# Four graph layers on one core: the diagonal of 15 row tiles multiplied by itself, and three or four column tiles whole there in place of six

## The chip, the core and the metric

The kernel runs on one core of a Trainium2 chip. The metric is the device time of one execution in microseconds (us). Three runs of the kernel before took 1402.44, 1414.2 and 1417.59 us; the median is 1414.2 us. A further execution was recorded by the hardware profiler, and every duration below comes from that one.

## What is computed

There are 2708 nodes with 512 features each, and one 2708 x 2708 matrix `adj` (float32, 45848 entries that are not zero, the whole diagonal among them, and denser towards low row and column numbers). Four layers follow one another; each begins with `h = relu(layernorm(x))` and ends with `x = x + layer(h)`:

```python
# layer 0: rows of adj plus a normalised mask, times h
head = (adj > 0) / sqrt(count of adj > 0 in the row)
inc  = adj + head;  out = (inc @ h) / inc.sum(-1)
# layer 1: attention with scores masked by (1 - max(adj, I)) * 1e16: in effect one node is picked per row
# layer 2: two graph convolutions and a projection
h = relu(adj @ (x @ W1) + b1);  h = relu(adj @ (h @ W3) + b3);  out = tanh(h @ Wf + bf)
# layer 3: mean over the nonzero pattern
A = (adj != 0);  out = (A @ (x @ W + b)) / A.sum(0)
```

So `adj`, or its pattern, is multiplied four times with a 2708 x 512 matrix.

## The kernel before

The nodes are cut into 22 row tiles of 128 (the last, number 21, has 20 rows). For a row tile m the product with `adj` has two parts. The first DENSE = 6 column tiles are taken **whole**: blocks of 128 x 128 are loaded from the transposed matrix and multiplied with the first six tiles of the right-hand side. Of the other columns only those that have an entry in any of the 128 rows are taken. They stand in a **list** for each row tile, cut in chunks of 128 (the table `CHUNKS`, 130 chunks in all): for each chunk GpSimd issues one indirect DMA that gathers the 128 entries of the matrix (`ac`, L576) and, in each later stage, one that gathers the 128 rows of the right-hand side (`gg`, L953; 256 KB each). Row tile 0 takes all columns whole. A list that doesn't fit sets a flag (`bad`, L406), and then a slow general path (from L1364) runs in addition.

The stages, in order, each a loop over row tiles:

- **Stage 0** (about 0 to 515 us): layer 0 and the lists. `row_norm` (L519) and `row_sum` (L537) read a slab of `adj` on ScalarE (ACT) three times: signs, their count, and a copy in place that sums the row. `count` (L265) adds up, on TensorE (PE), for three row tiles at once which columns are occupied; `rank_blocks` (L316) scans that on VectorE (DVE), the ranks are stored to HBM and loaded back spread over 128 partitions (`load_ranks`, L354), and `search` (L369) finds the listed columns. `attended` (L549) does the work of layer 1 on the slab. `incidence` (L627) builds `adj + head` from the blocks `at` and from the list; then PE multiplies (L791, float32), and `after` (L728) projects (`yacc`, L158).
- **Stage 1a** (about 515 to 650 us): `first_product` (L1066) for all 22 tiles, each with three products in float32r of four matmuls each (`project3`, L905), and row tile 0 of the first convolution.
- **Stage 1b** (about 650 to 950 us): the loop `for m in order_m` (L1096): `aggregate` (L957) and `aggregated` (L1024) for the other tiles, then one `project3` (L918).
- **Stage 2** (about 950 to 1310 us): the loop `for m in order_2` (L1285): the second convolution, again `aggregated`, then `project3` with Wf, tanh, the residual, a layernorm, and `project3` with W for layer 3; the result `go` is stored to `hid` (L1317) and without the first six tiles to `hidr` (L1320). Row tiles 1 to 5 come last.
- **Stage 3** (about 1310 to 1492 us): layer 3. Row tiles 0 to 3 take all columns whole (`full_steps`, L1252), the others six whole tiles (`whole_h`, L1200) and the list (`listed_products`, L1213; gathers from `hidr`). Each right-hand tile is split in two float32r halves, so each whole tile or chunk is two matmuls (L1193).

In stages 1b and 2 a whole tile is split in three float32r parts (`a_hi`, `a_lo`, `a_s`, L989 to L991) and costs three matmuls (L1002); a chunk of the list is one float32 matmul (L1005, two records in the profile). After the last one the two banks are added and the bias follows (`sum_banks` L879 and L880, then L1030), and `relu_parts` (L889) transposes the sum `u` on PE (L893).

What sets the order: each engine works through its own fixed list of instructions, written out by a scheduler ahead of time, and waits on semaphores. SyncE (SP) issues nearly all plain DMAs in one such list. Buffers come from pools: eight `gg` buffers for gathered rows, three `raw` for loaded blocks, two `u` (which in stage 2 hold the sum `u` and the tensor `z` in turn), two each of `agg`, `aggs`, `v_hi`, `v_lo`, `v_s`, and one each of `main` and `mixed`.

Of the kernel before, what the change touches and what calls it, by code (L numbers as in the profile page):

```python
# [9 lines left out]
FP = mybir.dt.float32  # L10
# [27 lines left out]
LEAD = 3  # L38
CHUNKS = (0, 10, 9, 8, 7, 7, 7, 7, 6, 6, 6, 6, 6, 6, 6, 5, 6, 5, 5, 5, 5, 2)


@with_exitstack
def kernel(
# [46 lines left out]
    def dense_of(m):  # L90

        return 0 if m == NT - 1 else DENSE

# [14 lines left out]
    hid = dram.tile([N + 1, D], FP, name="hid")  # L108
    hidr = dram.tile([N + 1 - DENSE * P, D], FP, name="hidr")
    y = dram.tile([N, D], FP, name="y")  # L110
# [15 lines left out]
    NGROUP = (NT + GROUP - 1) // GROUP  # L126
    BEHIND = DENSE * P
    WIDE, LOW = (N - BEHIND) // 4, BEHIND // 2
    assert WIDE * 4 == N - BEHIND and WIDE < BLK and LOW * 2 == BEHIND
    cnt_b = dram.tile([NGROUP + 1, P, WIDE], BF, name="cnt_b")  # L130
# [13 lines left out]

    rdeg = const.tile([P, NT], FP, name="rdeg")
    ones_b = const.tile([P, 1], BF, name="ones_b")
    nc.gpsimd.memset(ones_b, 1.0)
# [24 lines left out]

    def norm(pool, xt, n, dst, func=AF.Identity):

        stats = pool.tile([P, nc.vector.BN_STATS_DIM], FP, name="stats")
        nc.vector.bn_stats(stats[:n], xt[:n])
        mv = pool.tile([P, nc.vector.BN_AGGR_DIM], FP, name="mv")
        nc.vector.bn_aggr(mv[:n], stats[:n])
        rstd = pool.tile([P, 1], FP, name="rstd")
        nc.scalar.activation(rstd[:n], mv[:n, 1:2], AF.Sqrt, bias=eps[:n])  # L180
        nc.vector.reciprocal(rstd[:n], rstd[:n])
        shift = pool.tile([P, 1], FP, name="shift")
        nc.vector.tensor_scalar(
            shift[:n], mv[:n, 0:1], rstd[:n], -1.0, op0=ALU.mult, op1=ALU.mult
        )
        nc.scalar.activation(dst[:n], xt[:n], func, scale=rstd[:n], bias=shift[:n])
# [39 lines left out]
    with tc.tile_pool(name="l0_slab", bufs=2) as slabs, tc.tile_pool(  # L226
# [10 lines left out]
        for gd in (h0d, g1d, g2d, hid):  # L237
            nc.gpsimd.dma_start(out=gd[N:], in_=zero)
        nc.gpsimd.dma_start(out=hidr[N - DENSE * P :], in_=zero)

# [11 lines left out]
        for d in range(QUAD, P, QUAD):  # L252
            nc.vector.tensor_add(ahead_of[:, d:], ahead_of[:, d:], ident[:, : P - d])

        place_i = hp.tile([P, NCH], I32, name="place_i")
# [9 lines left out]
        def count(masks):  # L265

            ms = list(masks)
            r, g = len(ms), NGROUP if ms[0] == 0 else ms[0] // GROUP
            for num, w, first, dst in ((2, LOW, 0, cnt_l), (4, WIDE, BEHIND, cnt_b)):
                bank = ps_list.tile([P, BLK], FP, name="list")  # L270
                for b in range(num):
                    c0 = first + b * w
                    for i, m in enumerate(ms):
                        n = rows(m)
                        nc.tensor.matmul(
                            bank[b * QUAD : (b + 1) * QUAD, :w],
                            counts[:n, m % GROUP, :],
                            masks[m][:n, c0 : c0 + w],
                            start=(i == 0),
                            stop=(i == r - 1),  # L280
                        )
                k = num * QUAD
                t = hp.tile([P, w], BF, name=f"counts{num}")
                nc.scalar.copy(t[:k], bank[:k, :w])
                pending_c.append(
                    lambda t=t, k=k, dst=dst: nc.sync.dma_start(out=dst[g, :k], in_=t[:k])
                )
            return t

        def degrees():  # L290
# [4 lines left out]
            for t in range(NT):  # L295
# [7 lines left out]
                )  # L303
            nc.vector.reciprocal(rdeg[:, :NFULL], deg[:, :NFULL])
            if TAIL:
                nc.vector.reciprocal(rdeg[:TAIL, NFULL:], deg[:TAIL, NFULL:])

        def load_counts(g, r, dst):

            for num, w, first, src in ((2, LOW, 0, cnt_l), (4, WIDE, BEHIND, cnt_b)):  # L310
                nc.sync.dma_start(
                    out=dst[:, first : first + num * w].rearrange("i (b w) -> i b w", b=num),
                    in_=src[g, : num * QUAD].rearrange("(b i) w -> i b w", b=num)[:r],
                )

        def rank_blocks(ms, last_block):  # L316

            rk = hp.tile([P, WIDE], HF, name="rk")  # L320
            sums, offs = (wp.tile([P, 1], FP, name=name) for name in ("sums", "offs"))
# [6 lines left out]
            nc.vector.tensor_tensor_scan(rk, rk, rk, offs[:, 0:1], ALU.add, ALU.max)  # L328
            nc.sync.dma_start(out=rank_b[ms[0] // GROUP], in_=rk)

        def rank_rows(ms):
# [12 lines left out]
            if first:  # L344
                nc.sync.dma_start(
                    out=rank_b[m // GROUP].rearrange("(b i) w -> i b w", b=4)[:r],
                    in_=rank[:, first:].rearrange("i (b w) -> i b w", b=4),
                )
            else:
                nc.sync.dma_start(out=rank_l, in_=rank)  # L350
# [3 lines left out]
        def load_ranks(m):  # L354
            first = dense_of(m) * P
            num = N - first
            if first:
                ranks = slabs.tile([P, N + 1 - BEHIND], HF, name="ranks", bufs=2)
                q = m % GROUP

                row = rank_b[m // GROUP].rearrange("(b i) w -> i b w", b=4)[q : q + 1]
                nc.sync.dma_start(
                    out=ranks[:, :num].rearrange("p (b w) -> p b w", b=4),
                    in_=row.to_broadcast([P, 4, WIDE]),
                )
            else:
                ranks = in_slab()[:, : N + 1]
                nc.sync.dma_start(out=ranks[:, :N], in_=rank_l.to_broadcast([P, N]))
# [54 lines left out]
        def norm_h0(ts):  # L423
            for t in ts:
                n = rows(t)
                norm(wp, h0[t], n, h0[t], AF.Relu)
                nc.gpsimd.dma_start(out=h0d[span(t)], in_=h0[t][:n])
# [87 lines left out]
        def row_norm(m):  # L515
# [17 lines left out]
            if m not in LATE:  # L533
                flag_negative(m, sum_sgn, cnt)
            masks[m], row[m] = sgn, (rn, deg, cnt)

# [65 lines left out]

        PIECE0 = 6
        tiles_d = list(range(DENSE))
# [21 lines left out]
        def incidence(m):  # L626
# [20 lines left out]
            if m >= LEAD:  # L647
                pieces = [tiles_d] if dense_of(m) else []
            else:
                pieces = in_order if m + 1 < LEAD else dense_last  # L650
            for ts in pieces:
# [3 lines left out]
                add_head(inc[d], at[d], k, len(ts))  # L655
                pairs += [(inc[:k, i, :n], h0[t][:k]) for i, t in enumerate(ts)]
            if m >= LEAD:
                ac, gs = gathers.pop(m)
# [120 lines left out]
        for m in range(NT):  # L779
# [3 lines left out]
            if m + 2 < NT and m + 2 >= LEAD and dense_of(m + 2):  # L783
                blocks[m + 2] = load_block(m + 2, tiles_d)
            flush()
# [78 lines left out]

    order_2 = order_m[:1] + order_m[DENSE:] + order_m[1:DENSE]
    x3_last = dram.tile([P, D], FP, name="x3_last")
# [94 lines left out]
    def aggregate(m, parts, shifted, gd, marked):  # L961
# [13 lines left out]
        if num:  # L975
            ac = load_listed(m)
            chunks = [(ac[:, c, :], g) for c, g in enumerate(gather(m, gd))]
            if marked:
                mark(whole, ac)
        for ts in dense if dense_of(m) else []:  # L980
            gs = [parts(t) for t in ts]
# [12 lines left out]
            for i, t in enumerate(ts):  # L994
                ghi, glo, gs_ = gs[i]
                first, last = t == 0, t == DENSE - 1
                for acc, a, b, st, sp in (
# [26 lines left out]
    def aggregated(m, parts, shifted, gd, bias, marked=False):  # L1024
        n = rows(m)
        u = wp.tile([P, D], FP, name="u")
        main, mixed = aggregate(m, parts, shifted, gd, marked)
        if dense_of(m):
            sum_banks(u, main, mixed, n)
            nc.vector.tensor_add(u[:n], u[:n], bias[:n])  # L1030
        else:
# [167 lines left out]

    def whole_h(m, t0=0, t1=DENSE):  # L1200

        n = rows(m)
        t1 = min(t1, dense_of(m))
        for ts in (range(t, min(t + PIECE, t1)) for t in range(t0, t1, PIECE)):
            mask = ap.tile([P, PIECE, P], FR, name="a_hi" if t1 - t0 > 1 else "a_s")
            nc.vector.tensor_copy(
# [6 lines left out]
    def listed_products(m):  # L1213
# [4 lines left out]
        for c, g in enumerate(listed_h.pop(m)):  # L1218
            high = part_room()
            if m == order_3[0]:  # L1220

                behind(high[:1, :1], halves[DENSE - 2][0][:1, :1].bitcast(FP))
            for half in split_h(high, g, P):
# [59 lines left out]
    order_3.insert(NT // 2, NFULL)  # L1283
    FIRST = 2
    for m in order_2:  # L1285
        n = rows(m)
# [3 lines left out]
        if dense_of(m) and m not in FULL:  # L1290
            nc.vector.tensor_scalar_add(
                idx_h[:, m, : CHUNKS[m]], idx_g[:, m, : CHUNKS[m]], float(-DENSE * P)
            )
# [23 lines left out]
        nc.sync.dma_start(out=hid[span(m)], in_=go[:n])  # L1317
        if m >= DENSE:
            r0 = (m - DENSE) * P
            nc.sync.dma_start(out=hidr[r0 : r0 + n], in_=go[:n])  # L1320
        elif m == order_2[-1]:
# [3 lines left out]
            nc.vector.tensor_tensor(lo, go, hi.bitcast(FP), ALU.subtract)  # L1325
            halves[m] = hi, lo


# [3 lines left out]
    for k in order_3[:AHEAD]:  # L1332
        if k not in marks:
            gather_h(k)
        whole_h(k, 0, DENSE - 1)
    for i, m in enumerate(order_3):
        listed_products(m)
        if i < AHEAD:
            whole_h(m, DENSE - 1)
        finish_h(m)  # L1340
# [449 lines left out]
```

## Time and profile before

| what | value |
|---|---|
| median of three runs | 1414.2 us (1402.44 to 1417.59) |
| profiled execution | span 1491.9 us from first to last instruction; the page gives no other time for it |
| busy: PE, DVE, ACT, POOL (GpSimd) | 1301.6, 948.3, 689.1, 662.4 us |
| mean granted TensorE clock | 0.944 |
| DMA | 349.04 MB, 234 GB/s over the span |
| matmuls of whole tiles L1002 | 756 records (3 x 252) |
| matmuls of lists L1005 | 520 records (260 matmuls) |
| stage 0 matmuls L791, whole and listed | 348 and 222 records (174 and 111 matmuls) |

The profiled execution is 77.7 us (5.5%) longer than the median. Times are microseconds from the start of the span. A row of the timeline gives start, duration, engine, source line, operation, result<-operands and the number of instructions merged. A matmul's duration runs from its start to its modelled end, and the next one starts before that end; so the distance between two starts, not the duration, is what a matmul costs PE while it is never without work. In a table by stretches each engine has its busy time and, in brackets, its instructions, followed by granted clock, DMA share and GB/s.

### The profile page before, as it was taken

What the parts mean: (1) busy time and instruction counts of PE and PEld (TensorE: products, weight loads), DVE (VectorE), ACT (ScalarE), POOL (GpSimd) and SP (SyncE); (2) the same over time, 40 slices, a digit from 0 to 9 for tenths busy, and PEclk for the clock granted to TensorE, in tenths of its full rate; (3) what the DMA queues carried; (4) which work ended last, traced back from release to release, by engine and by line L of the source; (5) the groups of instructions that cost most, each with busy time, mean ns of one, the idle gap of its engine ahead of it and who ended that gap; (6) DMA issues with size and microseconds to landing.
All of it is one profiled execution on the core that took longest, in us unless ns stands there. A gap on an engine that the chain in (4) does not pass through costs nothing.

```text
span 1491.9 us, 15610 instructions
## 1 busy us (share of the span) xinstructions
PE 1301.6 (87%) x4478; PEld 774.6 (52%) x4478; DVE 948.3 (64%) x1944; ACT 689.1 (46%) x1051; POOL 662.4 (44%) x673
## 2 busy tenths in 40 slices
PE   4868777598898838988999999899999999879997
PEld 2323333243343326755665666466577666556766
DVE  4657777688899668743443445456566655558676
ACT  5856464353444446532323334245445544445453
POOL 1254454666585432044444443233433444535662
PEclk9988988899999869999999999899999999979999
DMA  9986787879798387466777777755565565748885
GB/s 341 349 272 223 243 289 256 295 233 332 226 328 317 107 288 261 157 198 218 244 235 215 239 236 235 262 167 170 161 196 164 180 210 185 226 134 280 271 248 165
DMA packets 196872, 349.04 MB, mean 234 GB/s; under 512 B 22198, under 2 KB 109840, under 8 KB 193045
## 3 DMA queue, kind: packets, MB, share of 16 engines
q1 hardware_dynamic: 149177, 200.80, 40.4%
q0 software_dynamic: 46032, 145.05, 31.2%
q10 hardware_dynamic: 1568, 2.10, 0.4%
q8 instruction: 37, 0.61, 0.2%
q14 instruction: 58, 0.48, 0.1%
HBM read 284.58 MB, written 63.29 MB: 233 GB/s over the span
## 4 chain that ended last, share of the span: by engine, by line
PE 68%; DMA 9%; DVE 7%; issue 7%; ACT 3%; another core or an unknown queue 2%; POOL 2%; SPq 1%; ACTq 0%; DVEq 0%; POOLq 0%
PE aggs L1005 14%; PE main L918 10%; PE acc L791 9%; PE agg L1002 7%; PE mixed L918 5%; PE aggs L1002 4%; PE yacc L158 3%; PE aggs L1193 3%; PE agg L1193 3%; PE pt L893 3%; PE aggs L1017 1%; PE pt L1193 1%; DMA lst<-ac 1%; PE agg L918 1%
## 5 line engine op out<-in xcount | busy, mean ns | idle before, releaser
L1005 PE MATMUL aggs<-gg,ac 128*128 128x512 f32 (+1 forms) x520 | 232.2, 594 | 3.6 <-DMA gg<-g1d,idx_g 3.6
L953 POOL DMA_INDIRECT gg<-g2d,idx_g x130 | 130.9, 1007 | 224.9 <-PE aggs L1005 175.7
L953 POOL DMA_INDIRECT gg<-g1d,idx_g x130 | 133.8, 1029 | 180.4 <-PE aggs L1005 109.3
L576 POOL DMA_INDIRECT ac<-in_adj_t_dram,idx_a x130 | 134.9, 1037 | 132.2 <-DMA lst<-ac 63.1
L791 PE MATMUL acc<-h,inc 128*128 128x512 f32 (+1 forms) x348 | 164.6, 615 | 18.1 <-DVE inc L644 10.3
L1005 PEld LDWEIGHTS aggs<-gg,ac 128*128 128x128 f32 (+1 forms) x520 | 97.6, 189 | 110.0 <-issue 102.2
L594 POOL DMA_INDIRECT h<-h0d,idx_g x111 | 115.3, 1038 | 51.7 <-issue 26.7
L158 PE MATMUL yacc<-wvo,hT 128*128 128x512 f32 (+1 forms) x176 | 92.8, 675 | 46.6 <-ACT hT L193 25.4
L1002 PE MATMUL agg<-ghi,a_hi 128*128 128x512 f32 x252 | 114.9, 456 | 8.6 <-ACT ghi L197 4.4
L989 ACT ACTIVATE a_hi<-raw 128x384 fp32r<-128x384 f32 x84 | 43.6, 520 | 160.5 <-issue 96.0
L791 PEld LDWEIGHTS acc<-h,inc 128*128 128x128 f32 (+1 forms) x348 | 64.9, 195 | 94.8 <-issue 78.8
L791 PE MATMUL acc<-h,incl 128*128 128x512 f32 (+1 forms) x222 | 103.5, 614 | 0.0
L1002 PE MATMUL agg<-glo,a_lo 128*128 128x512 f32 x252 | 101.8, 404 | 0.0
L1002 PE MATMUL aggs<-gs,a_s 128*128 128x512 f32 x252 | 100.2, 401 | 1.0 <-DVE gs L204 1.0
L990 DVE TENSOR_TENSOR a_lo<-raw,a_hi 128x384 fp32r<-128x384 f32 x84 | 47.4, 564 | 76.5 <-ACT a_hi L989 39.8
L899 DVE SCALAR_TENSOR_TENSOR v_lo<-pt,v_hi 128x512 fp32r<-128x512 f32 (+1 forms) x88 | 56.8, 664 | 48.9 <-issue 25.3
L158 PEld LDWEIGHTS yacc<-wvo,hT 128*128 128x128 f32 (+1 forms) x176 | 35.8, 213 | 97.6 <-issue 67.1
L953 POOL DMA_INDIRECT gg<-hidr,idx_h x62 | 63.0, 1016 | 49.8 <-PE aggs L1193 17.2
L880 DVE SCALAR_TENSOR_TENSOR u<-aggs,u 128x512 f32<-128x512 f32 x42 | 28.9, 687 | 77.3 <-PE aggs L1005 64.7
L898 ACT ACTIVATE v_hi<-pt 128x512 fp32r<-128x512 f32 (+1 forms) x88 | 49.1, 579 | 53.7 <-PE pt L893 38.5
L791 PEld LDWEIGHTS acc<-h,incl 128*128 128x128 f32 (+1 forms) x222 | 42.8, 196 | 52.3 <-issue 51.0
L556 DVE MAX8 top<-ar 128x8 f32<-128x2708 f32 (+1 forms) x22 | 65.4, 2972 | 0.1
(321 smaller groups left out, 2829.0 us busy)
## 6 DMA issues: line engine op xcount, KB each, us to landing
ar<-in_adj_dram SPq DMA_DIRECT2D x27, 1354.0 KB
raw<-in_adj_t_dram SPq DMA_DIRECT2D x122, 192.0 KB
slot<-x SPq DMA_DIRECT2D x41, 256.0 KB
at<-in_adj_t_dram SPq DMA_DIRECT2D x27, 384.0 KB
ranks<-rank_b SPq DMA_DIRECT2D x20, 485.0 KB
ac<-lst SPq DMA_DIRECT2D x16, 384.0 KB
h<-in_x_dram SPq DMA_DIRECT2D x21, 256.0 KB
h0d<-h POOLq DMA_DIRECT2D x21, 256.0 KB
```

Source lines behind the costliest of these rows:

```text
L158: nc.tensor.matmul(acc[:n], hT[:, c, :n], w[:, c, :], start=(c == 0), stop=(c == NCD - 1))
L556: nc.vector.max(top[:n], ar[:n])
L576: nc.gpsimd.indirect_dma_start(out=ac[:, c, :n], out_offset=None, in_=adj_units, in_offset=bass.IndirectOffsetOnAxis(ap=idx_a[:, m, c0 + c ...
L594: nc.gpsimd.indirect_dma_start(out=g, out_offset=None, in_=h0d[:, :], in_offset=bass.IndirectOffsetOnAxis(ap=idx_g[:, m, c : c + 1], axis=0),)
L791: nc.tensor.matmul(acc[:n], a, g, start=(i == 0), stop=(i == len(pairs) - 1))
L898: nc.scalar.activation(hi[d], pt[d], AF.Relu, scale=UP)
L899: nc.vector.scalar_tensor_tensor(lo[d], pt[d], 0.0, hi[d].bitcast(FP), op0=ALU.max, op1=ALU.subtract)
L918: nc.tensor.matmul(acc[:n], a[:, c, :n], b[:, c, :], start=first and c == 0, stop=last and c == NCD - 1,)
L953: nc.gpsimd.indirect_dma_start(out=gs[c], out_offset=None, in_=gd[:, :], in_offset=bass.IndirectOffsetOnAxis(ap=index[:, m, c : c + 1], ax ...
L1002: nc.tensor.matmul(acc[:n], a[:k, i, :n], b[:k], start=st, stop=sp)
L1005: nc.tensor.matmul(mixed[:n], a, g, start=(c == 0 and not dense_of(m)), stop=(c == len(chunks) - 1),)
L1193: nc.tensor.matmul(bank_h(m)[: rows(m)], a, b, start=(i == 1), stop=(i == total))
```

## The change

For row tiles 6 to 20 the entries on the diagonal are taken out of the occupation counts, so that a column which is occupied only by its diagonal entry no longer needs a place in the list. Its product is made apart: layer 0 gets one more float32 matmul of the identity with a scaled copy `own` of the row tile; stages 1b and 2 load the tile's own rows of the right-hand side (`u`, 256 KB by SP), multiply them by a column `diag_c` and add the bias before the banks are added; layer 3 adds the tile's own `go` times `self_w` to the residual. `diag_c` is zero where the column has other entries in the tile, and the list then carries the diagonal too.

With the shorter lists fewer column tiles stay whole: 4 in tiles 6 to 11 and 15 to 17, 3 in 12 to 14 and 18 to 20, six as before in 0 to 5. That is 36 whole tiles fewer in each of the four products; the number of chunks stays 130 (tile 8 has one more, tile 16 one fewer). The layout of counts and ranks now depends on the group of three tiles, the blocks of stage 0 come in pieces of four in place of six tiles, `sum_banks` and the addition of the bias in `aggregated` become two DVE operations, `hidr` leaves out three tiles in place of six, and in stage 2 row tiles 1 and 2 come last in place of 1 to 5.

```diff
-CHUNKS = (0, 10, 9, 8, 7, 7, 7, 7, 6, 6, 6, 6, 6, 6, 6, 5, 6, 5, 5, 5, 5, 2)
+HEAD = 3
+WHOLE = (6, 6, 6, 6, 6, 6, 4, 4, 4, 4, 4, 4, 3, 3, 3, 4, 4, 4, 3, 3, 3, 0)
+CHUNKS = (0, 10, 9, 8, 7, 7, 7, 7, 7, 6, 6, 6, 6, 6, 6, 5, 5, 5, 5, 5, 5, 2)
...
     def dense_of(m):
-        return 0 if m == NT - 1 else DENSE
+        return WHOLE[m]
+    def alone(m):
+        return DENSE <= m < NFULL
...
+    def layout(g):
+        first = (dense_of(g * GROUP) if g < NT // GROUP else DENSE) * P
+        return first, (N - first) // 4, first // 2
...
# row_norm
+            if alone(m):
+                cols = slice(m * P, (m + 1) * P)
+                nc.vector.tensor_tensor(sgn[:, cols], sgn[:, cols], off_diag, ALU.mult)
+                picked = wp.tile([P, P], FP, name="dg")
+                d = diag[:, m : m + 1]
+                nc.vector.scalar_tensor_tensor(
+                    picked, ar[:, cols], 1.0, ident, op0=ALU.mult, op1=ALU.mult, accum_out=d
+                )
+                others = ps_list.tile([P, BLK], FP, name="list")
+                nc.tensor.matmul(others[:, :1], sgn[:, cols], ones_b, start=True, stop=True)
+                nc.vector.scalar_tensor_tensor(
+                    diag_c[:, m : m + 1], others[:, :1], 0.0, d, op0=ALU.is_equal, op1=ALU.mult
+                )
...
-        PIECE0 = 6
+        PIECE0 = 4
...
# incidence
+            if alone(m):
+                c = diag_c[:, m : m + 1]
+                by = wp.tile([P, 3], FP, name="by")
+                nc.scalar.activation(by[:, 2:3], c, AF.Sign)
+                nc.scalar.activation(by[:, 2:3], by[:, 2:3], AF.Identity, scale=rn, bias=c)
+                nc.scalar.activation(by[:, :2], kept[:, :, m], AF.Copy, scale=by[:, 2:3])
+                own = wp.tile([P, D], FP, name="own")
+                nc.scalar.activation(own, xs[m], AF.Relu, scale=by[:, 0:1], bias=by[:, 1:2])
+                pairs.append((ident, own))
...
-    order_2 = order_m[:1] + order_m[DENSE:] + order_m[1:DENSE]
+    order_2 = order_m[:1] + order_m[HEAD:] + order_m[1:HEAD]
...
     def aggregated(m, parts, shifted, gd, bias, marked=False):
         n = rows(m)
         u = wp.tile([P, D], FP, name="u")
+        if alone(m):
+            nc.sync.dma_start(out=u, in_=gd[span(m)])
+            nc.vector.scalar_tensor_tensor(
+                u, u, diag_c[:, m : m + 1], bias, op0=ALU.mult, op1=ALU.add
+            )
+            bias = u
         main, mixed = aggregate(m, parts, shifted, gd, marked)
         if dense_of(m):
-            sum_banks(u, main, mixed, n)
-            nc.vector.tensor_add(u[:n], u[:n], bias[:n])
+            for bank, scale in ((main, 1.0 - EPS12), (mixed, EPS12)):
+                nc.vector.scalar_tensor_tensor(
+                    u[:n], bank[:n], scale, bias[:n], op0=ALU.mult, op1=ALU.add
+                )
+                bias = u
...
-        if m >= DENSE:
-            r0 = (m - DENSE) * P
+        if m >= HEAD:
+            r0 = (m - HEAD) * P
             nc.sync.dma_start(out=hidr[r0 : r0 + n], in_=go[:n])
...
+        if alone(m):
+            nc.vector.scalar_tensor_tensor(
+                xt, go, self_w[:, m : m + 1], xt, op0=ALU.mult, op1=ALU.add
+            )
```

## The prediction

> **What bounds the kernel now.** I read the page's busy shares and slices first, then the table by stretches, then the timeline of one row tile in stage 1b and one in stage 2, and the chain for transfers. Busy shares, then slices:
>
> ```profile
> PE 1301.6 (87%) x4478; PEld 774.6 (52%) x4478; DVE 948.3 (64%) x1944; ACT 689.1 (46%) x1051; POOL 662.4 (44%) x673
> ...
> PE   4868777598898838988999999899999999879997
> ...
> PEclk9988988899999869999999999899999999979999
> DMA  9986787879798387466777777755565565748885
> ```
>
> PE is full in the middle (stages 1b and 2), not in the first third. The table by stretches says who else is full where (PE, PEld, DVE, ACT, POOL, clock, DMA share, GB/s):
>
> ```profile
> 320.00:420.00 100.00, 87.09 (x238) 38.49 (x236) 85.27 (x181) 46.76 (x62) 63.94 (x60) 0.97 0.87 281
> 420.00:515.00 95.00, 83.08 (x202) 36.71 (x203) 90.14 (x172) 47.80 (x58) 57.81 (x53) 0.93 0.73 251
> ...
> 770.00:880.00 110.00, 107.52 (x388) 65.56 (x387) 44.80 (x75) 35.56 (x68) 49.78 (x49) 1.00 0.72 225
> ...
> 1100.00:1200.00 100.00, 99.93 (x393) 69.56 (x393) 66.67 (x122) 50.05 (x76) 36.33 (x36) 1.00 0.59 181
> ...
> 1360.00:1420.00 60.00, 55.32 (x228) 44.55 (x228) 42.07 (x79) 28.28 (x50) 38.49 (x37) 0.94 0.79 246
> 1420.00:1492.00 72.00, 61.76 (x253) 46.79 (x251) 49.80 (x94) 31.76 (x58) 29.86 (x29) 0.93 0.67 207
> ```
>
> Stage 0 is bound by PE and DVE alike, stages 1b and 2 by PE alone (98% and 100%), stage 3 mostly by PE. What a matmul costs there is read from starts, in stage 1b's timeline:
>
> ```profile
> 816.27 5.31 PE L1005 MATMUL aggs<-gg,ac 128*128 128x512 f32 x12
> ...
> 822.12 0.40 PE L1002 MATMUL agg<-ghi,a_hi 128*128 128x512 f32 x1
> 822.35 0.39 PE L1002 MATMUL agg<-glo,a_lo 128*128 128x512 f32 x1
> ...
> 829.18 5.31 PE L1005 MATMUL aggs<-gg,ac 128*128 128x512 f32 x12
> ```
>
> A row tile takes 12.9 us with PE never without work. Float32r matmuls start 0.229 us apart though each is shown as 0.4 us busy, so a whole tile costs 3 x 0.229 = 0.687 us; a listed chunk, two records, about 0.86 us. One row tile of stage 2, from its eight transposes to the next:
>
> ```profile
> 1098.49 1.04 PE L893 MATMUL pt<-ident,u 128*128 128x128 f32 x8
> ...
> 1104.58 0.32 SPq L1317 DMA_DIRECT2D hid<-go  x1
> 1104.95 0.42 SPq L1320 DMA_DIRECT2D hidr<-go  x1
> ...
> 1110.20 0.69 DVE L1309 TENSOR_TENSOR slot<-slot,u 128x512 f32<-128x512 f32 x1 [0.17 <-ACT u L1301]
> ...
> 1112.71 0.82 ACT L186 ACTIVATE u<-slot,shift,rstd 128x512 f32<-128x512 f32 x1 [0.54 <-DVE rstd L181]
> ...
> 1114.49 1.04 PE L893 MATMUL pt<-ident,u 128*128 128x128 f32 x8
> ```
>
> Here PE's work takes 16.0 us, but beside it runs a chain almost as long: projection, tanh, residual, layernorm, `z` ready at 1113.53, only 1.0 us before PE takes it. PE is the bound with one microsecond to spare; that is the point on which my forecast turns. Last, transfers of 256 KB in the chain:
>
> ```profile
> 1324.62 2.01 DMA hid<-go
> ...
> 1326.69 3.72 DMA glo<-hid
> ```
>
> A store took 2.01 us, a load 3.72 us, from the start of its issue.
>
> **Part by part.** The profiled execution is 77.7 us over the median. The chain shows 17.4, 13.3 and 15.0 us in stage 0 in which it waited for nothing the profile names (at 98, 218 and 280 us); I take all terms from other places and subtract them unscaled from the median, 1414.2.
>
> *Stage 0.* PE: 36 float32 matmuls fewer and 15 `own` ones more at 0.86 us is -18; the counts need some 60 more matmuls at 0.1 us (13 took 1.21 us), +6; together -12. DVE: three operations more for a diagonal at 0.28, 0.36 and 0.2 us, times 15, +13; `search` over 4608 more columns at 1.04 ns (2174 ns for 1941 columns, 2973 for 2709), +5; wider scans and ranks +1.5, more pieces in tiles 3 to 5 +2.5; `incidence` with 36 blocks fewer in two operations at 0.13 us (0.94 us for six, 0.54 for three), -10; together +12. ACT gains 15 x 1.4 = 21 us (a Relu of 0.81 and three of 0.2), hidden beside PE and DVE while ACT stays half busy. From 231 to 515 us PE is busy 243 us and DVE 240, equally near the bound, so half of each counts: 0. One wait is new: ACT's copy in place of the slab must let DVE read the diagonal first; 15 x 0.2 = +3. I take **+3**; bounds -12 (PE alone counts) and +20 (all of DVE's, and 0.5 us per wait).
>
> *Stage 1b.* 36 x 0.687 = -24.7. The `u` load, 256 KB, is issued a tile ahead in SP's list and lies under 11 us of PE work; behind it SP's next entries are loads for a later tile. DVE does one 0.69 us operation more per tile and ACT one 0.58 us less, both under half busy. Bytes per tile stay near 3.0 MB (+256 KB, -128 to -192 KB) in 11 to 12 us, 280 GB/s, as from 320 to 420 us, where the share was 0.87. Later landings may cost a tenth: +2.5. So **-22**; bounds -27 (the stage's 10.8 us of PE waits shrink a little) and -13 (PE idles 7.6% as it did from 652 to 770 us, in place of 1.5%, over some 190 us).
>
> *Stage 2.* PE again loses 24.7 us, 1.65 per tile; its work becomes 14.2 us a tile on average. But the changed order puts, on DVE, the operation that needs the loaded `u` ahead of the residual addition, and the two new bank operations ahead of and behind `BATCH_NORM_STATS2`, inside the chain. On SP the load stands behind the two stores of `go` from the projection just made. So, from the transposes at T: `go` is ready at T+6.1 to T+6.7 (1104.55, 1185.14), say 6.4; two stores issued, 0.9; the load lands L later; then DVE's `u` 0.72, residual 0.72, bank 0.71, stats 0.73, bank 0.71, and 1.91 from there to `z` (1111.62 to 1113.53), 0.1 for the wait: 5.6. Distance of transposes: 12.9 + L. By the store's 2.0, 14.9 us; by the 256 KB load's 3.72, 16.6; by 5.4 (the 384 KB load of `ac` at 821.61, used at 826.99), 18.3. Without any wait the chain alone gives 14.9: tanh done at T+10.1 (1189.07 less 1178.44, less one operation that went, with some slack), and then 4.8. Behind the waiting operation on DVE stand the residual, the layernorm and the splitting of the next blocks, so PE has little cover and waits at the transposes. I take L = 3.72, the row of the same size and direction: 15 x 16.6 = 249 against 15 x 16.0 less two chunks = 237.5, **+11**; bounds -14 and +37.
>
> The Trainium skill, "SBUF — State Buffer", section "The DMA setup-cost knee", puts a transfer at about 2 us plus its bytes over 436 GB/s, an estimate of 2.6 us here, well under the 3.72 us of the row; by it the distance would be 15.5 us, stage 2 would give -5 and the whole 1380. The measured load decides.
>
> *Stage 3.* 72 matmuls fewer at 0.227 us (12 in 2.72) is -16.3. Until 1420 us PE is 92% busy, after that 86% with the last tiles' ends; counting the first 45% fully (-7.4) and a third of the rest, **-10**; bounds -16 and 0. The `go` x `self_w` addition sits behind `go` in stage 2, 0.7 us of DVE time off the chain above. Stage 1a is unchanged.
>
> Sum: 3 - 22 + 11 - 10 = -18, so **1396 us**.
>
> **Rivals.** *Stage 2 keeps its saving.* If `u` lands within 2.0 us, or by T+9.4, the distance is 14.9 us and stage 2 gives -14: 1371 us. For it: DMA share there is only 0.59. Against: the load follows 512 KB of stores issued within a microsecond.
>
> *The gain is eaten.* If `u` lands as slowly as `ac`, 18.3 us a tile, +37: 1422 us, no change. For it: the stores ahead, and gathers of 250 KB beside it. Against: `ac` is 1.5 times as large.
>
> *Slower: stage 0's new wait.* ACT's copy in place waits for DVE's diagonal; where that stands behind `MAX8` and `FIND_INDEX8` (2.97 us each) it costs up to 5.9 x 15 = 89 us, and layer 0's divisor and ACT's later slabs move with it. It decides from about 2.3 us a tile (35 us in place of 3, sum +14). At 4 us: 60 - 3 = 57 more, 1453 us. Against: ACT is only half busy there, so much of a wait is slack.
>
> *The lists overflow* and the general path runs: the inputs' nonzero pattern excludes it (at most 855 of 896 places in tile 6, 579 of 640 in tile 15).
>
> **How the numbers follow.** My forecast 0.45, its own range 1385 to 1408; stage 2 keeps its saving 0.25; eaten 0.18; stage 0's wait 0.12. A change under 1% is about what a measurement of this kernel can't tell from none. Faster by over 1% means under 1400: 0.29 of the forecast's 0.45, the first rival's 0.25 and 0.02 of the second's, 0.56. Within 1%: 0.16 and 0.12 of the second's, less 0.01: 0.27. Slower: the last rival and 0.04 of the second, and a rest of 0.01, 0.17. The range 1362 to 1426 leaves out the slow rival (0.12) and 0.08 at its ends.
>
> **What would show it.** Stage 1b: distance between the listed groups 10.8 to 12.2 us with PE full. Stage 2: groups of eight transposes 16.6 us apart (14.9 and 18.3 for the rivals), PE idle ahead of them, and DVE's `u` waiting for the load from `g2d`. Stage 0 ending near 518 us, and ACT's copy waiting under 0.5 us for DVE. Matmuls of whole tiles in stages 1b and 2: 540 records in place of 756. Stage 2 running at 14.2 us, PE full, would prove the chain wrong; a shift of stage 0 by over 20 us either way, its terms.

## The result

| | median, us | runs |
|---|---|---|
| before | 1412.0 (1402.4 to 1417.6) | 6 |
| changed | 1463.9 (1448.6 to 1469.8) | 6 |

The ratio is 1.0359, with an interval of 1.0302 to 1.0417: 52 us slower, where 18 us faster were forecast.

One thing has to be known first. The same kernel before took about 1412 us on some chips and 1479 to 1489 us on others, and the profile that the prediction was read from (span 1491.9 us) was of the second sort: there single engines pause in stage 0 for up to 17 us with no releaser in the trace. A second profile of before (first experiment, span 1412.6) has no such pauses; the changed kernel's profile (1458.6) compares with that one. Where an experiment fell on a chip with pauses, its ratio to the kernel before on that chip is given.

### The profile page after: what moved, and what is told of

The parts are those of the page before. It is cut to its first block, busy times and chain, and to the rows that moved or that the text cites. A ratio compares the mean times of both kernels' runs of the same rounds, so it can differ in the third digit from the quotient of the medians.

```text
span 1458.6 us, 15175 instructions
## 1 busy us (share of the span) xinstructions
PE 1241.8 (85%) x4223; PEld 728.3 (50%) x4223; DVE 953.9 (65%) x2043; ACT 676.2 (46%) x1056; POOL 663.1 (45%) x674
## 5 line engine op out<-in xcount | busy, mean ns | idle before, releaser
L1077 PE MATMUL aggs<-gg,ac 128*128 128x512 f32 (+1 forms) x520 | 236.9, 598 | 4.7 <-DMA gg<-g1d,idx_g 4.7
L861 PE MATMUL acc<-h,inc 128*128 128x512 f32 (+1 forms) x276 | 140.5, 650 | 16.9 <-DVE inc L704 15.1
L654 POOL DMA_INDIRECT h<-h0d,idx_g x111 | 107.4, 968 | 66.5 <-PE acc L861 31.9
L1074 PE MATMUL agg<-ghi,a_hi 128*128 128x512 f32 x180 | 87.5, 486 | 24.6 <-DVE u L1108 20.9
L861 PEld LDWEIGHTS acc<-h,inc 128*128 128x128 f32 (+1 forms) x276 | 54.0, 207 | 81.0 <-issue 57.7
L1074 PE MATMUL agg<-glo,a_lo 128*128 128x512 f32 x180 | 79.6, 442 | 4.4 <-ACT glo L220 4.4
L1074 PE MATMUL aggs<-gs,a_s 128*128 128x512 f32 x180 | 75.3, 434 | 2.1 <-DVE gs L217 1.2
L571 ACT ACTIVATE sgn<-ar 128x2708 bf16<-128x2708 f32 (+1 forms) x22 | 54.1, 2457 | 32.4 <-DMA ar<-in_adj_dram 32.4
L618 DVE FIND_INDEX8 at_top<-top,ar 128x8 uint32<-128x2708 f32 (+1 forms) x22 | 65.3, 2970 | 0.0
L1061 ACT ACTIVATE a_hi<-raw 128x384 fp32r<-128x384 f32 (+1 forms) x72 | 33.4, 466 | 63.2 <-PE agg L1074 41.4
```

The costliest lines, as they stand in the source:

```text
L618: nc.vector.max_index(at_top[:n], top[:n], ar[:n])
L654: nc.gpsimd.indirect_dma_start(out=g, out_offset=None, in_=h0d[:, :], in_offset=bass.IndirectOffsetOnAxis(ap=idx_g[:, m, c : c + 1], axis=0),)
L861: nc.tensor.matmul(acc[:n], a, g, start=(i == 0), stop=(i == len(pairs) - 1))
L1074: nc.tensor.matmul(acc[:n], a[:k, i, :n], b[:k], start=st, stop=sp)
L1077: nc.tensor.matmul(mixed[:n], a, g, start=(c == 0 and not dense_of(m)), stop=(c == len(chunks) - 1),)
```

## The profile after

The changed kernel's page, its busy shares:

```profile
PE 1241.8 (85%) x4223; PEld 728.3 (50%) x4223; DVE 953.9 (65%) x2043; ACT 676.2 (46%) x1056; POOL 663.1 (45%) x674
```

PE is busy 40 us less than in the second profile of before (1282.1), and the kernel takes 46 us more, so PE is idle 86 us more. By the prediction's own terms PE's work should have fallen by 78 us (12, 24.7, 24.7 and 16.3), twice as much: the mean granted clock is 0.928 in place of 0.962, and the matmuls that are left take longer. The stretches below end at the last projection of layer 0, the first listed matmul of stage 1b, the first matmul of row tile 0 in the second convolution, and the last transposes. Before (second profile), then changed; columns as in the prediction's table:

```profile
0.00:470.00 470.00, 402.78 (x1142) 177.49 (x1142) 388.98 (x871) 267.50 (x341) 267.66 (x287) 0.95 0.88 302
470.00:605.00 135.00, 105.31 (x435) 74.60 (x435) 100.01 (x238) 72.26 (x137) 31.07 (x29) 0.90 0.68 226
605.00:878.00 273.00, 270.30 (x955) 166.40 (x956) 116.86 (x194) 90.08 (x167) 125.13 (x125) 0.99 0.75 239
878.00:1265.00 387.00, 368.41 (x1371) 242.78 (x1370) 229.02 (x428) 180.34 (x270) 157.42 (x157) 0.97 0.61 190
1265.00:1412.60 147.60, 135.29 (x578) 107.20 (x576) 110.14 (x214) 78.38 (x138) 80.73 (x77) 0.97 0.79 254
```

```profile
0.00:505.00 505.00, 404.11 (x1175) 177.02 (x1175) 394.69 (x955) 290.11 (x406) 265.48 (x289) 0.91 0.83 280
505.00:640.50 135.50, 106.63 (x433) 75.76 (x433) 100.58 (x239) 71.12 (x135) 30.76 (x26) 0.90 0.67 223
640.50:909.00 268.50, 251.18 (x850) 152.26 (x851) 114.22 (x199) 70.80 (x139) 122.85 (x127) 0.96 0.78 248
909.00:1312.00 403.00, 357.00 (x1261) 229.50 (x1260) 238.14 (x444) 164.91 (x241) 152.80 (x148) 0.93 0.59 182
1312.00:1458.00 146.00, 122.91 (x507) 93.72 (x505) 106.29 (x207) 79.25 (x138) 91.26 (x86) 0.94 0.82 269
```

| stretch | before | changed | difference | forecast |
|---|---|---|---|---|
| stage 0 | 469.6 | 504.9 | +35 | +3 |
| stage 1a | 135.4 | 135.6 | 0 | 0 |
| stage 1b | 273.5 | 268.9 | -5 | -22 |
| stage 2 | 386.5 | 402.7 | +16 | +11 |
| stage 3 | 147.6 | 146.5 | -1 | -10 |

In stages 1b to 3 PE's busy time falls, but stages 1b and 3 hardly shorten and stage 2 lengthens. In stage 1b an undisturbed tile is as short as forecast, 10.6 us with six chunks and three whole tiles (12.9 before with six whole tiles). PE's timeline of the changed kernel:

```profile
794.13 5.31 PE L1077 MATMUL aggs<-gg,ac 128*128 128x512 f32 x12
...
804.75 1.45 PE L1077 MATMUL aggs<-gg,ac 128*128 128x512 f32 x3
```

But not every tile is undisturbed. DVE, and PE's transposes of the same sum:

```profile
731.92 0.69 DVE L214 SCALAR_TENSOR_TENSOR glo<-slot,ghi 128x512 fp32r<-128x512 f32 x1 [8.16 <-ACT ghi L210]
732.53 0.68 DVE L1108 SCALAR_TENSOR_TENSOR u<-aggs,u 128x512 f32<-128x512 f32 x1
```

```profile
733.27 1.11 PE L963 MATMUL pt<-ident,u 128*128 128x128 f32 x4 [6.41 <-DVE u L1108]
```

DVE takes its operations in order: the read of the bank (L1108) stands behind the splitting of stage 2's right-hand side (L214), which waited 8.16 us for ScalarE and that for a load; PE, with its listed matmuls done by then, stood 6.4 us. In all PE waited 14.4 us in this stage for these reads.

Stage 2, one row tile from transposes to transposes:

```profile
1153.64 1.03 PE L963 MATMUL pt<-ident,u 128*128 128x128 f32 x8
...
1161.28 0.39 SPq L1100 DMA_DIRECT2D u<-g2d  x1
...
1164.16 0.75 DVE L1101 SCALAR_TENSOR_TENSOR u<-u,diag_c,bias 128x512 f32<-128x512 f32 x1 [0.98 <-DMA u<-g2d]
...
1165.43 0.68 DVE L1108 SCALAR_TENSOR_TENSOR u<-agg,u 128x512 f32<-128x512 f32 x1
...
1166.16 0.50 PE L1074 MATMUL agg<-ghi,a_hi 128*128 128x512 f32 x1 [1.08 <-DVE u L1108]
...
1171.59 0.60 PE L963 MATMUL pt<-ident,u 128*128 128x128 f32 x4
```

18.0 us here, 17.5 on average over six tiles from 1136.50 to 1241.62. The load takes 2.85 us, and DVE waits for it. PE stops not at the transposes but at the next tile's whole matmuls: they need the bank `agg`, which is free only when DVE has read it. DVE starts to read it 11.8 us after the transposes. Before, ScalarE did so 7.0 us after them:

```profile
1105.49 0.59 ACT L879 ACTIVATE u<-agg 128x512 f32<-128x512 f32 x1
```

PE goes on 12.5 us after the transposes here, and 11.8 to 12.6 us in all eight tiles that start from 1099 to 1223 us. The 5.4 us of whole and listed matmuls that follow end the cycle.

The wait costs more than its length. This is the shortest of those eight waits, 1.1 us, and the matmuls behind it start 0.23 us apart. In the other seven PE stood for 1.9 to 4.2 us, and behind each of them, at once or within 2 us, matmuls start about 0.43 us apart, for some three us:

```profile
1129.48 0.79 PE L1074 MATMUL agg<-ghi,a_hi 128*128 128x512 f32 x1 [2.78 <-DVE u L1108]
1130.06 0.63 PE L1074 MATMUL agg<-glo,a_lo 128*128 128x512 f32 x1
1130.49 0.63 PE L1074 MATMUL agg<-ghi,a_hi 128*128 128x512 f32 x1
```

The granted clock from 1130 to 1133 us is 0.51. In stage 2 PE's busy time falls by only 11 us, though whole matmuls worth 24.7 us have gone.

## Experiments

**The kernel before again**, unchanged.

> The kernel before, unchanged, for a second profile: the one shown spans 1491.9 us, where its other runs took 1402 to 1418 us. Expected: a span of 1400 to 1416 us, stage 2 still 16.0 us a row tile, stage 1b still 12.9 us for a tile with six chunks, and a stage 0 that ends some 30 to 45 us earlier than at 523 us, since the three long waits in which the chain showed no releaser all lay there.

1414.4 us, span 1412.6: the stages of the table above, 16.0 us a tile in stage 2 (from 1016.16 to 1112.01), stage 0 53 us shorter than in the first profile, more than the 30 to 45 expected. So what the prediction took for stage 0 held pauses beside the kernel's own time.

**Without the loaded rows in stages 1b and 2**, and **in stage 1b alone**:

```diff
-        if alone(m):
-            nc.sync.dma_start(out=u, in_=gd[span(m)])
-            nc.vector.scalar_tensor_tensor(u, u, diag_c[:, m : m + 1], bias, ...)
-            bias = u
```

> The changed kernel without the load of u and its product with diag_c in stages 1b and 2 (the diagonal's product is left out of the two convolutions; stage 0 and stage 3 are untouched). Theory 1, the loaded u stands ahead of DVE's reads of the two banks and so holds PE back: DVE waited 47.6 us for u in stage 1b and 9.1 us in stage 2, PE 14.4 us and 20.9 us for DVE's reads; without it the kernel takes 25 to 45 us less than the changed one's 1464, so 1420 to 1440. Theory 2, stage 0's new operations are the loss: it stays within 15 us of 1464.

> As the run before, but the load and its product are left out in stage 1b alone. Theory 1: 12 to 20 us under 1464, the rest of its effect belongs to stage 2, where the distance of the transposes stays near 17.5 us. Theory 2: no more than 8 us.

1436.5 us (ratio 1.0171, 1.0132 to 1.0211) and 1458.4 us (1.0339, 1.0304 to 1.0374). Stage 1b took 264.1 and 262.4 us in place of 268.9; stage 2 381.7 without the load and 406.9 with it, 14.9 us a tile from 1125.29 to 1199.82, where the changed kernel takes 17.3 for the same five tiles. The waiting operation on DVE costs about 21 us in stage 2 and 5 to 6 in stage 1b: theory 1 holds, but it explains half of the loss. In stage 2 the granted clock is back at 0.96 (0.93 in the changed kernel, 0.97 before). Even so stage 2 is only 5 us under before, since the layernorm's chain (14.9 us) then sets the distance. In stage 1b the load explains little: leaving it out there alone gave 5.5 us in all where theory 1 expected 12 to 20, and PE still waits 13.5 us for DVE's bank reads without it (first run; 9.1 in the second), with DVE's splitting behind ScalarE as before.

**Stage 0 bare:** only the mask on the occupation counts stays; the diagonal entry, the count of others, `diag_c` and `own` with its matmul go.

```diff
-                picked = wp.tile([P, P], FP, name="dg")
...
-                nc.vector.scalar_tensor_tensor(diag_c[:, m : m + 1], others[:, :1], 0.0, d, ...)
...
-                nc.scalar.activation(own, xs[m], AF.Relu, scale=by[:, 0:1], bias=by[:, 1:2])
-                pairs.append((ident, own))
```

> The changed kernel whose stage 0 only masks the diagonal out of the occupation counts: the diagonal entry, the count of others, the column diag_c and layer 0's own product are left out; diag_c stays zero, so stages 1b and 2 do the same work. Theory 2, the new operations and ACT's wait for DVE cost over 30 us: 1434 or less. Theory 1: 5 to 15 us less than 1464, as much as 15 matmuls of 0.86 us and two DVE operations are worth.

1416.6 us, ratio 1.000 (0.9965 to 1.0035). Stage 0 ends at 466.0 us, 39 earlier than in the changed kernel (the run profiled took 1424.2 us). Theory 2 holds too; if the two savings add up, 1464 less 28 less 47 would be 1389, but no run leaves both out. PE's waits from 100 us to the end of stage 0 show where to look, changed, then bare:

```profile
PE yacc L171 <- ACT hT L206: 28.2, 14, 6.8
...
PE list L591 <- DVE sgn L584: 9.2, 4, 4.6
```

```profile
PE yacc L171 <- ACT hT L206: 11.4, 9, 2.3
```

PE waits 17 us more for ScalarE's copy `hT`, 9 us for DVE's mask ahead of the count, and has 15 float32 matmuls more, 13 us at 0.86. That these make 39 is chance: the bare stage waits longer elsewhere (for `inc` 19.9 us in place of 12.8). By the whole stage PE is idle 17 us more and busy 22 us more (404.1 against 382.5), at a granted clock of 0.91 against 0.94. ScalarE's own waits in the changed kernel:

```profile
ACT own L725 <- DMA xt<-in_x_dram: 48.2, 10, 6.9
```

The operation that forms `own` reads the tile's rows of x, whose load was timed for the residual at the tile's end. ScalarE's copy in place of the slab, the wait that my last rival named, has no wait in this list.

**Own from other data, rows loaded early, own rows ahead, both.** The first reads row tile 0 in place of the tile's rows; the second loads the rows one tile earlier; the third loads the tile's own rows one tile ahead into two buffers (the `gg` buffers become six in place of eight) and adds them between the two bank reads:

```diff
-                nc.scalar.activation(own, xs[m], AF.Relu, ...)
+                nc.scalar.activation(own, h0[0], AF.Relu, ...)
```

```diff
-            if m + 1 < NT:
-                load_x(m + 1)
+            if m + 2 < NT:
+                load_x(m + 2)
```

```diff
+        load_own(order_2, m, g2d)
         parts = aggregated(m, second_parts, second_product, g2d, bias3)
...
                 bias = u
+                if bank is main and alone(m):
+                    nc.vector.scalar_tensor_tensor(
+                        u, own_rows.pop(m), diag_c[:, m : m + 1], u, op0=ALU.mult, op1=ALU.add
+                    )
```

> The changed kernel whose layer 0 forms own from row tile 0, which has been in SBUF since the start, in place of the tile's own rows (the diagonal's product of layer 0 is made of the wrong rows; instructions and their number are the same). The bare stage 0 was 39 us shorter (466.0 against 504.9), more than its work. Theory 2a, the operation on ScalarE that forms own waits for the load of the tile's rows (48.2 us over ten tiles in the changed kernel) and everything behind it on ScalarE waits too: stage 0 ends 25 to 39 us earlier, the kernel takes 1425 to 1440 us. Theory 2b, the loss is the 21 us of ScalarE's and 13 us of VectorE's new work and ScalarE's wait for the diagonal to be read: within 12 us of 1464.

> The changed kernel that loads each row tile's rows one tile earlier in stage 0 (a fourth buffer for them, one buffer for own in place of two). Theory 2a: as the run before, 1425 to 1445 us, stage 0 ending at 466 to 485 us. Theory 2b: within 12 us of 1464.

> The changed kernel whose stages 1b and 2 load the tile's own rows one row tile earlier into two buffers of their own (the gathered rows get six buffers in place of eight) and add them between the reads of the two banks, so that nothing that waits for a transfer stands ahead of the reads on VectorE, and neither read stands inside the chain of the layernorm. Theory 1: like the run without the load, 1430 to 1445 us, stage 2's distance of transposes back to 15 to 16 us. If the two buffers were what PE lived on, PE waits for gathers and it is 1464 or more.

> The last two edits together. Theories 1 and 2a, which act in different stages, add up: 1464 less 20 to 35 less 20 to 35, so 1395 to 1424 us; below 1400 it beats the kernel before.

Before took 1489.1 us on this chip. Ratios: 1.0215 (1.0105 to 1.0324); 1.024 by the medians, without an interval; 1.0139 (1.0055 to 1.0223); 1.0034 (0.9972 to 1.0097). Stage 0 held pauses of some 15 us in each, so the first two say nothing of it. Stage 2 can be read; own rows ahead:

```profile
1210.77 1.04 PE L963 MATMUL pt<-ident,u 128*128 128x128 f32 x8
...
1217.39 0.68 DVE L1110 SCALAR_TENSOR_TENSOR u<-agg,bias 128x512 f32<-128x512 f32 x1
...
1218.13 0.50 PE L1074 MATMUL agg<-ghi,a_hi 128*128 128x512 f32 x1 [0.18 <-DVE u L1110]
...
1225.98 1.09 PE L963 MATMUL pt<-ident,u 128*128 128x128 f32 x8
```

The bank is read 6.6 us after the transposes, PE waits 0.2 us, a tile takes 15.2 us. The whole of stage 2 takes 389.8 us at a clock of 0.97; the first profile of before, also with pauses, has 395.3 there. With the diagonal still computed, that is as good as leaving the load out: the loss was that the bank's read stood behind a wait in DVE's order, not the transfer or the sum as such. Loading earlier and adding later were changed together, so their shares stay open.

**The changed kernel again, and stage 0's parts one by one.** The second run is own from other data again; the third leaves the count of others out:

```diff
-                others = ps_list.tile([P, BLK], FP, name="list")
-                nc.tensor.matmul(others[:, :1], sgn[:, cols], ones_b, start=True, stop=True)
...
-                    diag_c[:, m : m + 1], others[:, :1], 0.0, d, op0=ALU.is_equal, op1=ALU.mult
+                    diag_c[:, m : m + 1], d, 0.0, d, op0=ALU.not_equal, op1=ALU.mult
```

> The changed kernel, unchanged, as the measure for the three runs beside it: the last four ran on a chip on which the kernel before took 1489 us in place of 1412, with pauses of all engines in stage 0, so that their times compare with nothing shown earlier. Expected: the ratio of 1.036 to the kernel before again, stage 0 ending 30 to 40 us later than in it.

> The changed kernel whose layer 0 forms own from row tile 0, which is in SBUF, in place of the tile's own rows (layer 0's diagonal product is made of the wrong rows). PE waited 30.4 us for ScalarE's copy hT in stage 0 with own as it is, 11.4 us without any of it. Theory 2a, own's wait for the rows' load on ScalarE is most of stage 0's loss: 20 to 30 us under the changed kernel beside it. Theory 2c, the count of others is: under 10 us.

> The changed kernel without the matmul that counts a column's other entries in the tile (15 of 0.17 us): diag_c takes the diagonal entry whatever else its column holds, so such a diagonal is counted twice. That matmul stands in PE's list ahead of listed matmuls and waits for DVE's masking, 10.7 us in stage 0. Theory 2c, that wait is the loss: 20 to 35 us under the changed kernel. Theory 2a: 5 to 12 us.

> Both edits of the two runs before. If the two waits are all of stage 0's loss beyond its work, 30 to 39 us under the changed kernel, as with the bare stage 0; if what remains is the work of the new operations, they give 15 to 25 us and the rest stays.

Before took 1485.1 us. Ratios 1.0249 (1.0179 to 1.0319), 1.0251 (1.0171 to 1.0331), 1.041 (1.0341 to 1.0479), 1.0282 (1.018 to 1.0384). Inconclusive: stage 0 ended at 558, 522, 546 and 559 us, by its pauses. The changed kernel's own ratio, expected at 1.036, was 1.0249 here, and the ratio of own from other data was the same (1.0251).

> Layer 0 forms own from row tile 0, which is in SBUF, in place of the tile's own rows (a wrong diagonal product in layer 0). Where the kernel before takes about 1412 us, stage 0 of the changed kernel ended at 505 us in three profiles and at 466 without its new operations. There PE waited 19 us more for ScalarE's copy hT, 11 us for DVE ahead of the count of others, and had 13 us more work. Theory 2a (ScalarE late because own waits for its rows): stage 0 ends at 480 to 490 us, the kernel takes 1440 to 1450. If own's wait is covered anyway: 500 to 508 us. Should the kernel before take 1480 us or more, pauses of single engines without a releaser hide a difference of this size.

> Without the matmul that counts a column's other entries in the tile (diag_c takes every diagonal entry, so such a diagonal is counted twice). Theory 2c, that matmul's place in PE's list costs what PE waited ahead of it: stage 0 ends at 493 to 499 us, 1450 to 1458 for the kernel; no difference if those waits only stand in place of later ones.

> Both edits of the two runs before. The sum by the waits: stage 0 ends at 470 to 480 us, 1430 to 1442 for the kernel; what then lies between it and the bare stage 0's 466 us is the work of 15 matmuls and of the operations on DVE and ScalarE.

> The changed kernel with the rows of x loaded one tile earlier in stage 0 and the tile's own rows loaded one tile ahead in stages 1b and 2, added between the reads of the banks. Stage 2 without the load gave back 21 us, stage 1b 5 to 6, own's wait up to 25: 1410 to 1435 us where the kernel before takes 1412; below 1400 it would beat it.

Again with pauses (before 1478.8 us): 1.0126 (1.0072 to 1.018), 1.0262 (1.0192 to 1.0331), 1.032 by the medians, and 1.0068 (1.0024 to 1.0112). Leaving the count out was no gain on the chip before, where the changed kernel ran beside it (1.041 against 1.0249); here it was slower than own from other data (1.0262 against 1.0126), and no changed kernel ran beside them. Nothing supports theory 2c.

> The version with both kinds of rows loaded ahead, once more, for a chip on which stage 0 has no pauses (the kernel before at about 1412 us). There theory 2a expects stage 0 to end at 480 to 492 us in place of 505 and the kernel to take 1405 to 1430 us; if own's wait was covered, stage 0 ends at 500 to 508 and the kernel takes 1430 to 1445.

1.0126 (1.0077 to 1.0176), before at 1489.0 us. The version with both loads ahead gave 1.0034, 1.0068 and 1.0126, all on chips with pauses: it takes back most of the loss and doesn't beat the kernel before.

> The last run: layer 0 forms own from row tile 0, which is in SBUF, in place of the tile's own rows (a wrong diagonal product in layer 0). On a chip without pauses in stage 0, theory 2a expects stage 0 to end at 480 to 490 us in place of 505 and the kernel to take 1440 to 1450; if ScalarE's wait is covered by other work, 500 to 508 and 1455 to 1466. On a chip with pauses it can't be read, and the cause within stage 0 stays open.

Here before took 1410.2 us, without pauses: 1455.1 us, ratio 1.0321 (1.0282 to 1.0359), and stage 0 ends at 492.1, against 504.9, 505.5 and 506.2 in the three profiles with that stage as it is and no pauses. So ScalarE's wait for the rows is worth 13 us of the 39 in stage 0, half of what theory 2a expected at the least in the first of these runs. The kernel as a whole gained only 9 us, since stages 1b and 3 took 5 and 3 us longer, and its interval overlaps the changed kernel's (1.0302 to 1.0417). ScalarE then waits at the same operation for something else:

```profile
ACT own L725 <- PE acc L861: 21.7, 7, 5.8
```

and PE for ScalarE's copy less, but still more than in the bare stage:

```profile
PE yacc L171 <- ACT hT L206: 18.4, 14, 4.6
```

`own` has two buffers, and PE's matmul gives them back late. Of the other 26 us, 13 are as much as the 15 matmuls are long; how the rest divides between these buffers, the count, DVE's operations and the lower clock stays open.

## Why the prediction was wrong

- *Stage 0, +3, was +35: the step that failed.* "ACT gains 15 x 1.4 = 21 us [...] hidden beside PE and DVE while ACT stays half busy": cost and engine load were right (ScalarE is busy 23 us more), but the operation reads rows that arrive late, and an engine that is half busy still works in order: 48.2 us of waits, some of which reached PE through `hT`. Taking these waits away shortened the stage by 13 us, taking all the new operations away by 39; the rest is measured only as a sum. And PE's 15 new matmuls were set off against the 36 that went; the bare stage 0, with these 36 gone as well, is only 3.6 us shorter than before, so the 36 were worth little beyond what the mask and the longer counts cost.
- *The last rival* had the right stage, but names a wait that the trace doesn't show; that its turning point, 35 us, is also the measured shift is luck.
- *Stage 1b, -22, was -5.* The price of a tile's work is right (10.6 us). What went wrong is "with PE full": DVE's bank reads stood behind its waiting operations, and PE waited 14.4 us for them. The `u` load, which should lie "under 11 us of PE work", kept DVE waiting 47.6 us, but only 5 to 6 us of the stage go with it; without it 9 to 11 us of the 24.7 came back. The splitting of loaded rows held the reads with and without the load. The clock was 0.96 against 0.99, 0.97 to 0.98 without the load. What the rest is made of stays open.
- *Stage 2, +11, was +16.* The load on DVE ahead of the chain, and the sign, were right; the chain without it is 14.9 us as worked out. The load took 2.85 us and not 3.72, and with that the prediction's own terms put the end of the bank's read at T+12.3 and the distance at 15.75 us. The read did end there (PE went on at T+11.8 to T+12.6). What was left out is the branch that starts there: PE's whole and listed matmuls, 5.4 us, wait for this read, and 12.1 and 5.4 make the 17.5 us measured. The fall of the clock behind PE's waits was left out as well, in every stage: all matmuls were priced at the distance they have while PE never waits. (In the sum, 240 less two chunks is 238.3 and not 237.5; the term stays at +11.)
- The transfer by the Trainium skill ("SBUF — State Buffer", "The DMA setup-cost knee"), an estimate of 2.6 us, was nearer to the 2.85 us measured than the row I took.
- *Stage 3, -10, was -1.* PE's busy time fell 12 us and the stage hardly: PE's waits for other engines rose from 5 to 15 us, the longest of them for DVE's `a_hi` (8.4 us, 4.5 before). No run separates why.
- The profile was read as if its stage 0 were the kernel's. Its three long waits without releaser were noticed and left out of the terms, rightly: the second profile has none of them.

## What to carry to other kernels

Before calling an operation on a half-idle, in-order engine free, look up when its inputs arrive and what stands behind it. A buffer's last reader sets when the next writer may start: moving that read from ScalarE to a place behind a transfer on DVE cost 21 us in stage 2, where the matmuls taken away gained 5 without it. A wait of PE can cost more than its length: in stage 2 here matmuls ran at about half their rate for some three us behind waits of 1.9 us and more. Matmuls taken from a stage shorten it only as far as the next chain, which here lay 1 us below.

## What was not expected of the hardware

The half rate of matmuls behind PE's waits, shown above, was not looked for. And the same program took 1410 to 1412 us in three of the sessions, on at least two chips, and 1479 to 1489 us in four others, on other chips. Between the two profiles of before, 53 of the 79 us lie in stage 0, in pauses without a releaser, as ScalarE's below in the run with own rows ahead; stages 1b, 2 and 3 are each some 8 us longer too. No run shows why, nor whether it is the chip, since no chip is known to have run in two sessions:

```profile
473.97 0.60 ACT L206 ACTIVATE hT<-pt 128x512 f32<-128x512 f32 x1 [16.01 <-remote]
```
